# Delta rule: upper triangles of the decays by a selection by index on GpSimd, in place of products with a matrix of ones and zeros

## Chip, cores and metric

The kernel runs on one core of a Trainium2 chip. The metric is the device time of one execution in microseconds, as the median of several runs. One further execution was taken with the hardware profiler; its own time is given beside its span below, and all durations of single instructions come from it.

## What is computed

The program is a block of four residual layers on x of shape (8, 512, 256) in float32: a gated recurrence with an MLP, a mixture of experts, a gated delta rule and an attention over chosen tokens. The change touches the delta rule alone. There, for each batch and each of 8 heads (keys of 128, values of 64), the reference runs over 512 tokens

```python
def step(state, inp):
    q_t, k_t, v_t, a_t, b_t = inp
    retained = jnp.einsum('bhvk,bhk->bhv', state, k_t)
    rk = retained[..., None] * k_t[:, :, None, :]
    vk = v_t[..., None] * k_t[:, :, None, :]
    state = a4 * (state - b4 * rk) + b4 * vk
    o_t = jnp.einsum('bhvk,bhk->bhv', state, q_t)
```

with decays alpha = exp(g), where g is negative and comes from the token by a projection and a softplus; a4 and b4 are a_t and b_t with two axes added. Queries and keys are normed to length one, and the outputs are normed, gated and projected.

## The kernel before, in words

The tokens of a batch are cut into NT = 4 chunks of P = 128. Inside a chunk the recurrence is written with matrices: a strictly triangular matrix of key products, weighted by decays, is inverted, and the state is carried from chunk to chunk. Heads go in groups of HG = 4, so there are 16 groups (8 batches with 2 groups each), the loop over n near L1074.

The work of a group lies in generators, and a list of letters (`order`, L1059) says which generator is taken one step further at each point; in one turn of the loop over n, group n is advanced (`advance`, a; `sides`, v; `silus`, g; `outputs`, o), group n+1 is prepared and inverted (`prepare`, p; `inverses`, i), and the channels, norms and decays of group n+2 are made (`channels`, c; `norms`, n; `fade`, e). Rows of the next batch are loaded at even or odd n by `load` (t, l), which issues gathers from GpSimd (L1027) and adds them on VectorE (L1031). Each engine runs its own queue in order.

- `fade` (L721) makes, for each chunk t, the decays between all pairs of tokens of that chunk, for four heads side by side, in the tile e (128 partitions by 4 x 128). L728 on GpSimd multiplies le, which is one where the column is at or above the row and zero below, with g repeated along the columns. L730 on TensorE multiplies with gt (ones where the row is above the column), which sums g over the tokens between; L731 on ScalarE takes the exponential; L732 on GpSimd multiplies with le again, so that the lower triangle is zero. A group has four of each, so there are 64 of each in all.
- `prepare` (L736) multiplies the key and query products of a chunk (L746, TensorE) with e and a factor on VectorE (L748) and writes NQ. Its last reading of an e frees the tile for the group after.
- `inverses` (L751) inverts the triangular part of NQ. First blocks of 8 and 16 on VectorE, by many small instructions from SBUF to SBUF (L779, L789, L793, L794, L802, L803, L816, L817), then two transposes on VectorE (L763: dn and up), then larger blocks by matmuls on TensorE, from L831 on, which begin with dn.
- `advance` (L930) carries the state: products with the state (L950), VectorE (L952, L953), the product with the inverse (L957), ScalarE (L959), and the new state (L965 on GpSimd, L968 on TensorE, L970 or L972 on VectorE).
- `outputs` (L984) multiplies the gates with the outputs on GpSimd (L990).

The tile le is made once at the start of the program, by the operation that the change uses (`affine`, L69 and L70), and is also read by a matmul in `decays` (L666). Other uses of that operation are on tiles of 4, 8 and 128 elements with one loop in the pattern.

Of the kernel before, what the change touches and what calls it, by code (L numbers as in the profile page):

```python
# [16 lines left out]
ALU = mybir.AluOpType  # L17
# [3 lines left out]
P = 128  # L21
# [11 lines left out]
HG = 4  # L33
# [3 lines left out]
def bc(ap, axis, n):  # L37

    ap = ap.unsqueeze(axis)
    shape = list(ap.shape)  # L40
    shape[axis] = n
    return ap.to_broadcast(shape)
# [3 lines left out]
def block(ctx: ExitStack, tc: tile.TileContext, a: dict, out: bass.AP):  # L46
    nc = tc.nc
    V, S, G, TE = nc.vector, nc.scalar, nc.gpsimd, nc.tensor
# [4 lines left out]
    def cst(shape, name):  # L53
        return const.tile(shape, F32, name=name, tag=name)
# [18 lines left out]
    le = cst([P, P], "le")  # L73
# [492 lines left out]
    def delta_rule():  # L566
        with ExitStack() as cx:
# [153 lines left out]
            def fade(s):  # L721


                b, hg, hs = s.b, s.hg, s.hs
                s.es = []
                for t in range(NT):
                    e = un.tile([P, HG, P], F32, name=f"e{b}_{hg}_{t}", tag="e", bufs=NT)
                    G.tensor_mul(e, bc(le, 1, HG), bc(s.g[:, t, hs], 2, P))  # L728
                    pe = pa.tile([P, HG, P], F32, name=f"pe{b}_{hg}_{t}", tag="pa")
                    TE.matmul(pe, gt, e, start=True, stop=True)  # L730
                    S.activation(e, pe, AF.Exp)  # L731
                    G.tensor_mul(e, e, bc(le, 1, HG))  # L732
                    s.es.append(e)
                    yield

# [309 lines left out]
            def group(n):  # L1045

                b, hg = divmod(n, H1 // HG)
                return SimpleNamespace(**vars(seqs[b]), hg=hg, hs=slice(hg * HG, (hg + 1) * HG))
# [17 lines left out]
            for n in range(2):  # L1066
                s = groups[n] = group(n)
                drain(channels(s), norms(s), fade(s))
                if n == 0:
                    drain(prepare(s), inverses(s))  # L1070
# [3 lines left out]
            for n in range(total):  # L1074
                s, s1 = groups.pop(n), groups.get(n + 1)
# [316 lines left out]
```

## Time and profile before

| what | value |
|---|---|
| median of 3 runs | 3373.59 us (3373.55 to 3381.02) |
| the profiled execution | 3381.53 us, span 3379.8 us |
| mean granted TensorE clock | 0.910 |
| TensorE, VectorE, ScalarE, GpSimd busy | 3018.4, 1900.5, 1548.0, 574.0 us |
| delta rule, from first channels to last output | about 1490 to 2907 us of the span |
| L731, exponential on ScalarE, 128x512 | 64, mean 596 ns |
| L748, NQ on VectorE, 128x256 | 256, mean 477 ns |
| TensorE idle from 1545 to 2910 us, summed | 142.9 us |

How to read the lines of the profile: PE is TensorE, PEld its weight load, DVE VectorE, ACT ScalarE, POOL GpSimd. A row of a group gives line, engine, operation, output and inputs, shape and count, then the busy time in us and the mean of one in ns, and after the second bar the engine's idle time ahead of these instructions and what ended it. A row of the waits gives who waited for whom, the us in total, how often and the longest. A row of a timeline gives the start in us from the begin of the span, the duration of the merged piece, engine, line, operation and, in brackets, the idle time ahead of it with what ended it. Spans on GpSimd are rough.

### The profile page before, as it was taken

How to read it: one execution, taken by the hardware profiler on the slowest of the kernel's cores; microseconds unless marked ns; L12 is line 12 of the kernel's file. 1: busy time of each engine (PE TensorE's matmuls, PEld its weight loads, DVE VectorE, ACT ScalarE, POOL GpSimd, SP SyncE). 2: the span in 40 equal slices, each digit the busy share in tenths (PEclk: the TensorE clock that was granted, in tenths of full speed). 3: DMA queues.
4: the chain of work that ended last, by engine and by line, in shares of the span. 5: the costliest groups of instructions: out<-in, count | busy, mean ns of one | idle time of the engine just before them, and what ended most of it. 6: DMA issues, size and time to landing. Idle time of an engine off the chain costs nothing.

```text
span 3379.8 us, 59439 instructions
## 1 busy us (share of the span) xinstructions
PE 3018.4 (89%) x24662; PEld 2227.4 (66%) x24662; DVE 1900.5 (56%) x4415; ACT 1548.0 (46%) x2747; POOL 574.0 (17%) x629
## 2 busy tenths in 40 slices
PE   7999999979999999977899898898989999498887
PEld 3655555535999999973566666666666667365664
DVE  4555545534555555556467767767677664554432
ACT  3554442212333333325466666767666663233322
POOL 1000001320000111014122222312121110212111
PEclk8999998989999999998789898989989896698787
DMA  5000003220788888871000000000000000201111
GB/s 205 13 25 13 13 13 148 69 67 19 271 337 330 330 327 320 327 284 31 2 1 20 8 20 8 26 2 26 2 23 2 8 2 8 94 23 42 36 40 47
DMA packets 97133, 302.69 MB, mean 90 GB/s; under 512 B 12760, under 2 KB 79456, under 8 KB 87648
## 3 DMA queue, kind: packets, MB, share of 16 engines
q0 software_dynamic: 19440, 221.19, 17.4%
q1 hardware_dynamic: 68016, 68.44, 6.0%
q10 hardware_dynamic: 9408, 9.27, 0.8%
q8 instruction: 194, 3.18, 0.4%
q14 instruction: 75, 0.61, 0.1%
HBM read 248.79 MB, written 50.08 MB: 88 GB/s over the span
## 4 chain that ended last, share of the span: by engine, by line
PE 69%; DVE 12%; DMA 11%; issue 4%; ACT 2%; POOL 2%; SPq 0%; another core or an unknown queue 0%; ACTq 0%; POOLq 0%; DVEq 0%
PE p_r L444 13%; PE pc L681 8%; DMA zbuf<-bz,rows 5%; PE pp L304 3%; PE pk L746 3%; PE pj L399 3%; PE pyr L522 3%; PE pkq L950 3%; DMA w<-in_experts,wrow 2%; PE pf L394 2%; PE p_s L444 2%; PE py L1008 2%; PE st L1271 2%; PE pw L957 1%; DVE cy L685 1%
## 5 line engine op out<-in xcount | busy, mean ns | idle before, releaser
L444 PE MATMUL p_r<-zT,w 128*128 128x128 f32 x4544 | 533.0, 275 | 6.1 <-DMA w<-in_experts,wrow 5.5
L444 PEld LDWEIGHTS p_r<-zT,w 128*128 128x128 f32 x4544 | 525.0, 192 | 11.6 <-issue 7.1
L685 DVE SCALAR_TENSOR_TENSOR cy<-pc,conv,cy 128x509 f32<-128x509 f32 (+2 forms) x480 | 351.4, 740 | 139.7 <-ACT cy L683 134.6
L448 ACT ACTIVATE t_r<-p_r,w 128x128 f32<-128x128 f32 x568 | 170.9, 374 | 263.5 <-PE p_r L444 183.9
L444 PE MATMUL p_s<-sxT,shared_w 128*128 128x512 f32 x512 | 226.2, 603 | 22.1 <-DVE l_s L449 20.4
L444 PEld LDWEIGHTS p_s<-sxT,shared_w 128*128 128x128 f32 x512 | 98.1, 193 | 145.6 <-issue 106.3
L508 POOL DMA_INDIRECT w<-in_experts,wrow x71 | 66.8, 940 | 676.3 <-ACT sg_r L457 655.8
L449 DVE SCALAR_TENSOR_TENSOR l_r<-p_r,w,t_r 128x128 f32<-128x128 f32 x284 | 80.0, 344 | 175.7 <-PE p_r L444 175.7
L681 PE MATMUL pc<-cxT,wq 128*128 128x512 f32 x256 | 150.8, 714 | 15.0 <-DVE cy L685 12.9
L681 PE MATMUL pc<-cxT,wk 128*128 128x512 f32 x256 | 146.0, 665 | 6.1 <-DVE cy L685 3.7
L304 PE MATMUL pp<-hT,win 128*128 128x512 f32 x320 | 142.9, 598 | 0.2 <-ACT hT L126 0.2
L522 PE MATMUL pyr<-w,htr 128*128 128x256 f32 x568 | 136.0, 383 | 2.6 <-DVE htr L462 2.6
L683 ACT ACTIVATE cy<-pc,conv 128x512 f32<-128x512 f32 x160 | 108.4, 686 | 62.3 <-PE pc L681 61.0
L449 DVE SCALAR_TENSOR_TENSOR g_r<-p_r,w,t_r 128x128 f32<-128x128 f32 x284 | 79.9, 344 | 98.8 <-PE p_r L444 98.8
L746 PE MATMUL pk<-kq 128*128 128x256 f32 x512 | 130.2, 391 | 0.7 <-DVE NQ L748 0.4
L728 POOL TENSOR_TENSOR e<-le,g 128x512 f32<-128x512 f32 x64 | 66.3, 1042 | 364.2 <-DVE NQ L748 341.6
L748 DVE SCALAR_TENSOR_TENSOR NQ<-pk,nbk,e 128x256 f32<-128x256 f32 x256 | 110.0, 477 | 27.2 <-PE pk L746 26.8
L394 PE MATMUL pf<-hT,fc 128*128 128x512 f32 x256 | 121.5, 601 | 0.0
L457 ACT ACTIVATE sg_r<-g_r 128x512 f32<-128x512 f32 x71 | 44.8, 631 | 159.9 <-DVE g_r L455 159.9
L399 PE MATMUL pj<-pj,sT 128*128 128x256 f32 x512 | 113.1, 379 | 0.0
L522 PEld LDWEIGHTS pyr<-w,htr 128*128 128x128 f32 x568 | 103.6, 192 | 14.2 <-issue 2.7
L950 PEld LDWEIGHTS pkq<-state,kq 128*128 128x128 f32 x768 | 95.4, 197 | 24.2 <-DVE state L972 16.7
(393 smaller groups left out, 6179.0 us busy)
## 6 DMA issues: line engine op xcount, KB each, us to landing
zt<-zbuf SPq DMA_DIRECT2D x71, 128.0 KB
ybuf<-yt SPq DMA_DIRECT2D x71, 128.0 KB
zbuf<-zeros SPq DMA_DIRECT2D x11, 768.0 KB
x<-in_x SPq DMA_DIRECT2D x8, 512.0 KB
xbuf<-x SPq DMA_DIRECT2D x8, 512.0 KB
sx<-xbuf SPq DMA_DIRECT2D x8, 512.0 KB
xbuf<-sx SPq DMA_DIRECT2D x8, 512.0 KB
cx<-xbuf SPq DMA_DIRECT2D x8, 512.0 KB
```

Source lines behind the costliest of these rows:

```text
L304: TE.matmul(ps, win[:, k, m : m + P], hT[:, k, :], start=k == 0, stop=k == DK - 1)
L394: TE.matmul(ps, fc[:, k, f * P : (f + 1) * P], hT2[:, k, :], start=k == 0, stop=k == DK - 1)
L399: TE.matmul(ps, sT[:, f, t * P : (t + 1) * P], pj[:, f, :], start=f == 0, stop=f == 7)
L444: last_of[0] = TE.matmul(ps[:, f, :], wx[:, k, (f0 + f) * P : (f0 + f + 1) * P], xin[:, k, :], start=k == 0, stop=k == DK - 1)
L448: S.activation(t3[:, f, :], p3[:, f, :], AF.Identity, bias=b3[:, f0 + f : f0 + f + 1])
L449: V.scalar_tensor_tensor(t1[:, f, :], p1[:, f, :], b1[:, f0 + f : f0 + f + 1], t3[:, f, :], ALU.add, ALU.mult)
L522: last_of[0] = TE.matmul(ps, hT[:, f, :], w2[:, f, :], start=f == 0, stop=f == 3)
L681: TE.matmul(ps, w[:, k, n * P : (n + 1) * P], xT[:, k, :], start=k == 0, stop=k == DK - 1)
L685: V.scalar_tensor_tensor(y[:, j:], ps[:, : T - j], conv[:, at + n, 3 - j : 4 - j], y[:, j:], ALU.mult, ALU.add)
L746: TE.matmul(pk[:, j, :, :], kq[:, h + j, 0, ts], kq[:, h + j, :, ts], start=True, stop=True)
L748: V.scalar_tensor_tensor(NQ[:, :, t * HG + h + j, :], pk[:, j, :, :], s.nbk[:, t, h + j : h + j + 1], bc(e[:, h + j, :], 1, 2), ALU.mult, ...
L950: TE.matmul(ps[:, n, h, :], s.kq[:, h, n, ts], state[:, h, :], start=True, stop=True)
```

## The change

Both products with le become selections by index on GpSimd: element (p, h, j) of the output is the input where j - p is zero or more, and 0.0 elsewhere. The first reads g repeated along the columns by a zero step, the second works on e in place. Each now reads one tensor; before, each read two.

```diff
                 b, hg, hs = s.b, s.hg, s.hs
                 s.es = []
+
+                def upper(dst, src):
+
+                    G.affine_select(out=dst, in_=src, pattern=[[0, HG], [1, P]], compare_op=ALU.is_ge, fill=0.0, base=0, channel_multiplier=-1)
+
                 for t in range(NT):
                     e = un.tile([P, HG, P], F32, name=f"e{b}_{hg}_{t}", tag="e", bufs=NT)
-                    G.tensor_mul(e, bc(le, 1, HG), bc(s.g[:, t, hs], 2, P))
+                    upper(e, bc(s.g[:, t, hs], 2, P))
                     pe = pa.tile([P, HG, P], F32, name=f"pe{b}_{hg}_{t}", tag="pa")
                     TE.matmul(pe, gt, e, start=True, stop=True)
                     S.activation(e, pe, AF.Exp)
-                    G.tensor_mul(e, e, bc(le, 1, HG))
+                    upper(e, e)
                     s.es.append(e)
                     yield
```

## Prediction

> **What bounds the kernel now.** I read first the busy shares and the chain of waits on the page, then TensorE's waits inside the delta rule (1550 to 2760 us), then GpSimd's groups, then the timelines of two neighbouring steps of the group loop, engine beside engine.
>
> ```profile
> PE 3018.4 (89%) x24662; PEld 2227.4 (66%) x24662; DVE 1900.5 (56%) x4415; ACT 1548.0 (46%) x2747; POOL 574.0 (17%) x629
> ```
> TensorE is the bound and GpSimd, which alone is edited, is busy 17%. In the chain of the delta rule GpSimd stands only ahead of 1563 us (four L728 in a row, 4.02 us, and two gathers). Time saved on GpSimd itself is thus worth almost nothing; the question is what its instructions do to others.
>
> ```profile
> PE pn L831 <- DVE dn L763: 45.7, 6, 8.4
> ...
> PE pkq L950 <- DVE state L972: 11.2, 8, 1.6
> ```
> Both long waits of TensorE end at VectorE, in the inverses of the group ahead (L763 is their transpose) or behind them in VectorE's queue (L972). So I look at why VectorE is late there. A step whose turn loads rows (even n), first VectorE, then GpSimd, then TensorE:
>
> ```profile
> 2182.63 1.25 DVE L779 SCALAR_TENSOR_TENSOR L<-low,front 128x256 f32<-128x256 f32 x1
> ...
> 2186.96 1.83 DVE L793 TENSOR_TENSOR p<-L,inv 128x72 f32<-128x72 f32 x1
> ...
> 2194.28 1.22 DVE L816 TENSOR_SCALAR both<-inv,front 128x256 f32<-128x256 f32 x1
> 2195.42 1.35 DVE L817 TENSOR_SCALAR both<-inv,second 128x256 f32<-128x256 f32 x1
> ```
> ```profile
> 2182.32 1.27 POOL L732 TENSOR_TENSOR e<-e,le 128x512 f32<-128x512 f32 x1
> ...
> 2187.37 1.28 POOL L732 TENSOR_TENSOR e<-e,le 128x512 f32<-128x512 f32 x1
> ...
> 2194.07 2.54 POOL L732 TENSOR_TENSOR e<-e,le 128x512 f32<-128x512 f32 x2
> ```
> ```profile
> 2197.44 1.91 PE L831 MATMUL pn<-dn,NQ 32*32 32x16 f32 x128 [8.19 <-DVE dn L763]
> ```
> And the next step (odd n), VectorE and TensorE:
>
> ```profile
> 2259.27 1.07 DVE L793 TENSOR_TENSOR p<-L,inv 128x98 f32<-128x98 f32 x1
> ...
> 2260.66 1.84 DVE L802 TENSOR_TENSOR pm<-L,inv 128x512 f32<-128x512 f32 x1
> ...
> 2269.82 0.34 DVE L816 TENSOR_SCALAR both<-inv,front 128x256 f32<-128x256 f32 x1
> ```
> ```profile
> 2265.37 2.81 PE L950 MATMUL pkq<-state,kq 128*128 128x64 f32 x16 [1.58 <-DVE state L972]
> ```
> The same L816 takes 0.34 us where no L732 runs and 1.22 us beside one. Each of the long VectorE instructions ends 0.1 to 0.3 us behind the end of an L732 (2183.88 against 2183.59; 2188.79 against 2188.65; 2195.50 against about 2195.35): it doesn't run slowly, it stands until the product is done. Their clean times in the same views: L779 0.47, the 72-element L793 0.28, L816 and L817 0.34, the 98-element L793 0.32, pm 0.99. The lost time is 0.78 + 1.55 + 0.88 + 1.01 = 4.2 us in a full even step, and 0.5 (an 8-element L793, 0.73) + 0.75 + 0.85 = 2.1 us in an odd one; over the loop I count some 48 such cases and 41 us. VectorE instructions that read PSUM (L685, L748, L952) keep their times beside L732 and L728. That is the cost the edit can reach: not the product's own time but the time for which VectorE's SBUF-to-SBUF instructions stand.
>
> **The change, part by part.** It replaces 64 L728 and 64 L732 one for one. Built, the order of TensorE, VectorE, ScalarE and SyncE is the same instruction for instruction with the same waits, and GpSimd's too apart from the operation; no wait and no DMA is added or moved. The tile le stays (the matmul of L666 reads it).
>
> ```profile
> L732 POOL TENSOR_TENSOR e<-e,le 128x512 f32<-128x512 f32 x64 | 81.3, 1277 | 53.8 <-ACT e L731 53.7
> ...
> L728 POOL TENSOR_TENSOR e<-le,g 128x512 f32<-128x512 f32 x64 | 66.3, 1042 | 364.2 <-DVE NQ L748 341.6 <-DVE g L663 18.8 <-DVE mvc L110 2.6
> ...
> L1297 POOL COPY full<-den 128x512 f32<-128x512 f32 x16 | 9.3, 607 | 59.7 <-DVE den L1294 56.9 <-DVE ahead L1185 2.8
> ...
> L70 POOL TENSOR_SCALAR_AFFINE_SELECT heads<-heads 128x8 f32<-128x8 f32 x2 | 0.4, 200 | 0.0
> ...
> L70 POOL TENSOR_SCALAR_AFFINE_SELECT gt<-gt 128x128 f32<-128x128 f32 x1 | 0.3, 289 | 0.0
> ```
> Price of a new select. The trace has it at 8 and at 128 elements: (289 - 200)/120 = 0.74 ns an element, so 200 + 504 x 0.74 = 574 ns at 512. A one-input copy at 512 takes 607 ns, its source repeated by a zero step as g is here. I take 0.61. The old rows have one loop; the new pattern has two, [0,4] and [1,128]. If each row of 128 paid the whole price again it would be 4 x 289 = 1156 ns. Bounds: 0.57 and 1.16. The one rule that speaks against the change: the Trainium skill, "GPSIMD Engine Reference", Performance versus the Vector engine, puts data-dependent branching at about 12 cycles an element; at its 1.2 GHz that is an estimate of 5.1 us for 512 elements, four times the product, and over 100 us slower in all. The 0.74 ns slope is under one such cycle, so the operation does not branch by element; the row decides.
>
> Does it still make VectorE stand? The trace has no select beside an SBUF-reading VectorE instruction. The Trainium skill, "SBUF — State Buffer", SBUF: two separate sides, says that the pair of ports that VectorE and GpSimd share is locked for the whole instruction, against two-input or two-port VectorE instructions, by a GpSimd instruction that reads SBUF; a select reads SBUF, so by the rule the stall gets shorter, not nothing. Every stall above fits that. By the rule: 0.67 us off per L732 met. Without lock: all 4.2 and 2.1 us. I take the rule; the other end is a rival.
>
> Even step, walked through: L779 stands to the end of the first select. GpSimd reaches it 0.43 us earlier too (L728 ahead of it 1.04 to 0.61), so 0.78 is saved, all of the stall. L793 saves 0.67 of its 1.55. The gathers between wait for VectorE (L1031 frees their buffers) and shift with it. Then the pair: 2.54 becomes 1.22, and L816 and L817 end some 1.35 earlier. Sum 2.8 us, on the path: dn follows, and TensorE waits for nothing else (ScalarE's L814 waits for the same L803 and needs 0.62, less than L816 and L817 need). The gap of 8.2 becomes 5.4; next late is still dn. There are five such gaps (8.17, 8.38, 8.19, 8.17, 8.18): 14.0 us. A sixth, 4.64 with two stalls: 1.4. The first step, around 1705, with three stalls of 0.45, 0.50 and 0.86: 1.3.
>
> Odd step: the selects follow ScalarE's exponentials, not VectorE; VectorE gains some 0.5, 0.5 and 0.85 at its three stalls, 1.8 us at L972, more than the gap of TensorE ahead of L950 (1.29 once, 1.58 six times). The gaps close: 10.8 us. Next late is TensorE's own queue.
>
> Clock: behind four of these seven gaps the granted clock is at a half for 3.4, 3.4, 6.8 and 3.4 us (2266.35 to 2273.18 in the step shown, with TensorE busy throughout), 17 us that cost 8.5. If three quarters of that goes, 6 us. I add nothing behind the even gaps: 5.4 us of idleness will still halve the clock.
>
> Start: the four L728 at 1547.95 end 1.7 us earlier, but the gather behind them also waits for a VectorE L1031 that starts at 1551.04 (stands 0.74 us beside L728): 0.8 us.
>
> GpSimd's remaining saving, 81.3 + 66.3 - 128 x 0.61 = 69.5 us of busy time, is counted at nothing: it sits idle 364 us ahead of L728 alone. Nothing is queued later than before, so no cover is lost.
>
> Sum: 14.0 + 1.4 + 1.3 + 10.8 + 6 + 0.8 = 34 us. I take 32, as closed gaps may uncover a ScalarE wait (its table loads fill the odd step). The profiled execution took 3381.5 (span 3379.8 and 1.7 around it), so 3349.5 in its terms; it lies 8 us above the median of 3373.6, which gives 3342.
>
> **The rivals.**
> 1. The lock shortened, as above: 3342, some 12 to either side. Chance 0.62.
> 2. The select doesn't lock VectorE out, or more half-clock stretches vanish: even steps 5 x 4.2 + 1.8 + 1.7, odd 10.8, clock 8.5 and more, start 0.8, together about 47 to 55: 3318 to 3327. For it: no overlap was traced. Against: the rule, and the copy's like nature. Chance 0.13.
> 3. Little changes: the two-loop pattern restarts at each row and takes 1.16. Then 0.12 us goes from each L732 and 0.11 is added to each L728, which blocks nothing in the loop: 4 x 5 + 4 + 7 x 3 = 45 stalls on the path by 0.12, 5 us: 3368. A wait of ScalarE's in place of VectorE's would end near it. Chance 0.13.
> 4. Slower: the second loop is counted in software and costs at each element. From 1.28 us on, VectorE stands longer than today; 45 us of path for each further us of select. At 2.0 us it is 0.72 x 45 = 32 us: 3406. For it: no row has two loops. Against: the slope and the copy of 512 with two loops at 607. Chance 0.12.
>
> **How the numbers follow.** About 0.3%, 10 us, is what a measurement of this kernel can tell from no change. Rivals 1 and 2 are faster by more than that but for the upper edge of 1 (0.02): 0.73. Same: 0.13 and that edge, 0.15. Slower: 0.12. The range takes in 1 and 2 and the near part of 3: 3318 to 3366.
>
> **What would show it.** Right: select rows near 0.6 us in place of 1277 and 1042 ns; the 72-element L793 near 1.2 us, L817 near 0.9 or less; TensorE's wait for dn some 14 to 17 us less in total, that for L972 near nothing. Wrong: select rows above 1.1 us; or short rows and short VectorE instructions with TensorE waiting as long, for ScalarE. VectorE instructions at their clean times beside a select would say that there is no lock.

## The result and the profile after

| what | before | after |
|---|---|---|
| median of 4 runs each, same chip | 3375.74 us (3373.55 to 3381.02) | 3340.25 us (3335.47 to 3341.52) |
| ratio to before, 95% interval | 1 | 0.9892 [0.9876, 0.9907] |
| profiled execution, its span | 3381.53, 3379.8 us | 3341.52, 3339.8 us |
| mean granted clock | 0.910 | 0.915 |

The changed kernel is faster by 35.5 us; 3342 was forecast. Measured again beside the second group of experiments below, it gave 3337.39 us, 0.9894 [0.9875, 0.9913]. Its lines behind the edit stand five further down: L779 is now L784, L793 is L798, L802 is L807, L816 and L817 are L821 and L822, L831 is L836, L950 is L955, L763 is L768, L972 is L977, L1027 and L1031 are L1032 and L1036. Both selections have the line of their helper, L729; "e<-g" is the first, "e<-e" the second.

The busy line of the page, after:

```profile
PE 3002.4 (90%) x24662; PEld 2219.1 (66%) x24662; DVE 1864.6 (56%) x4415; ACT 1546.3 (46%) x2747; POOL 507.4 (15%) x629
```
The counts are the same. VectorE ran the same 4415 instructions in 36 us less: these are, to within a microsecond or two, the us for which they no longer stand (34.6 of them in the loop below). GpSimd is 67 us less busy. TensorE, with as many matmuls, is 16 us less busy, which I put down to its clock.

GpSimd's two groups, after:

```profile
L729 POOL TENSOR_SCALAR_AFFINE_SELECT e<-e 128x512 f32<-128x512 f32 x64 | 42.4, 669 | 66.4 <-ACT e L736 66.4
L729 POOL TENSOR_SCALAR_AFFINE_SELECT e<-g 128x512 f32<-128x512 f32 x64 | 40.2, 636 | 374.2 <-DVE NQ L753 351.8 <-DVE g L663 21.4
```
A selection takes 0.64 to 0.67 us where the products took 1.28 and 1.04. Neither of the dearer prices that the prediction weighed is seen: 1.16 us with a restart at each row of 128, or a price by element that would have made it 5.1 us.

The even step shown before, in the kernel after: VectorE, then GpSimd, then TensorE (timelines: start, duration, engine, line).

```profile
2169.31 0.48 DVE L784 SCALAR_TENSOR_TENSOR L<-low,front 128x256 f32<-128x256 f32 x1
...
2172.88 0.53 DVE L798 TENSOR_TENSOR p<-L,inv 128x72 f32<-128x72 f32 x1
...
2175.12 0.48 DVE L1039 SCALAR_TENSOR_TENSOR cx<-yg,wts,cx 128x256 f32<-128x256 f32 x1 [0.62 <-DMA yg<-ybuf,rows]
...
2179.82 0.57 DVE L821 TENSOR_SCALAR both<-inv,front 128x256 f32<-128x256 f32 x1
2180.31 0.72 DVE L822 TENSOR_SCALAR both<-inv,second 128x256 f32<-128x256 f32 x1
```
```profile
2168.59 0.63 POOL L729 TENSOR_SCALAR_AFFINE_SELECT e<-e 128x512 f32<-128x512 f32 x1
...
2172.29 0.97 POOL L1032 DMA_INDIRECT yg<-ybuf,rows  x1 [0.31 <-DVE p L798]
2173.27 0.64 POOL L729 TENSOR_SCALAR_AFFINE_SELECT e<-e 128x512 f32<-128x512 f32 x1
...
2179.62 1.27 POOL L729 TENSOR_SCALAR_AFFINE_SELECT e<-e 128x512 f32<-128x512 f32 x2
```
```profile
2181.70 1.90 PE L836 MATMUL pn<-dn,NQ 32*32 32x16 f32 x128 [5.77 <-DVE dn L768]
```
L784 is at its clean time, because the selection ahead of it ends at 2169.22, before L784 starts at 2169.31. L798 of 72 elements went from 1.83 to 0.53. L821 and L822 still stand, for 0.23 and 0.37 us, beside the two selections that end at 2180.89: VectorE still stands, for a shorter time. TensorE's gap went from 8.19 to 5.77. A new wait of 0.62 us for the landing of a gather is in VectorE's queue.

The odd step after, VectorE and TensorE:

```profile
2242.93 0.33 DVE L798 TENSOR_TENSOR p<-L,inv 128x98 f32<-128x98 f32 x1
...
2243.59 1.08 DVE L807 TENSOR_TENSOR pm<-L,inv 128x512 f32<-128x512 f32 x1
```
```profile
2247.82 1.89 PE L955 MATMUL pkq<-state,kq 128*128 128x64 f32 x16
```
Both long VectorE instructions (1.07 and 1.84 before) are clean or nearly so, and TensorE reaches L955 without a gap; the same sixteen matmuls take 1.89 us in place of 2.81, at full clock.

TensorE's waits from 1545 to 2730 us of the kernel after (us in total, times, longest), which takes in the same waits as the prediction's lines:

```profile
PE pn L836 <- DVE dn L768: 32.1, 7, 5.8
...
PE pkq L955 <- DVE state L977: 0.5, 1, 0.5
```
45.7 became 32.1 and 11.2 became 0.5. The five large gaps went from 8.17, 8.38, 8.19, 8.17 and 8.18 to 5.83, 5.74, 5.77, 5.75 and 5.75, the sixth from 4.64 to 2.95.

Last the loop as one stretch, from the first L831 of the first group to that of the fifteenth, before and after. The columns are the stretch, its length, TensorE's busy time, its weight loads, VectorE, ScalarE, GpSimd, the granted clock, the DMA share and GB/s.

```profile
1623.10:2754.00 1130.90, 1028.66 (x12571) 750.16 (x12571) 772.64 (x1633) 749.15 (x1105) 264.84 (x265) 0.91 0.04 11
```
```profile
1625.50:2723.20 1097.70, 1015.64 (x12566) 744.18 (x12566) 738.03 (x1633) 748.12 (x1105) 203.82 (x265) 0.92 0.04 11
```
The loop is 33.2 us shorter: TensorE is idle 20.2 us less (102.2 to 82.1) and busy 13.0 us less. By the slices of the clock, 213 us of the stretch ran at half clock before and 181 after. The stretch ahead of it, from the first channel matmul to the first L831, is 0.9 us shorter too (91.7 to 90.8), but it is 89.1 to 91.5 us in the other kernels of the first two groups below, with the old product there or without, so this is within its scatter. The stretch from the first L831 of the sixteenth group to the last output matmul is 7 us shorter (81.3 to 73.9), but that isn't the change's: see the first experiment.

### The profile page after: what moved, and what is told of

Read it like the earlier page. It is cut to its first block, busy times and chain, and to the rows that moved or that the text cites. A ratio compares the mean times of both kernels' runs of the same rounds, so it can differ in the third digit from the quotient of the medians.

```text
span 3339.8 us, 59439 instructions
## 1 busy us (share of the span) xinstructions
PE 3002.4 (90%) x24662; PEld 2219.1 (66%) x24662; DVE 1864.6 (56%) x4415; ACT 1546.3 (46%) x2747; POOL 507.4 (15%) x629
## 4 chain that ended last, share of the span: by engine, by line
PE 39%; DVE 7%; DMA 3%; issue 3%; ACT 2%; POOL 1%; another core or an unknown queue 0%; POOLq 0%; DVEq 0%; ACTq 0%; SPq 0%
PE pc L681 8%; PE pk L751 3%; PE pkq L955 3%; PE py L1013 2%; PE pg L929 2%; PE pw L962 2%; PE st L1276 1%; PE sc L1255 1%; PE pow L981 1%; PE pst L973 1%; PE pn L881 1%; PE pe L735 1%; PE pu L890 1%; PE pn L701 1%; DMA yg<-ybuf,rows 1%
## 5 line engine op out<-in xcount | busy, mean ns | idle before, releaser
L1255 PE MATMUL sc<-dk,dq 32*128 32x256 f32 x512 | 80.4, 532 | 30.0 <-DVE maxs L1257 25.8
L304 PEld LDWEIGHTS pp<-hT,win 128*128 128x128 f32 x320 | 60.1, 192 | 70.9 <-issue 66.5
```

The costliest lines, as they stand in the source:

```text
L304: TE.matmul(ps, win[:, k, m : m + P], hT[:, k, :], start=k == 0, stop=k == DK - 1)
L1255: TE.matmul(sc[r][:, j, :], qT[rs, 2 * m + j, qs], kT[rs, 2 * m + j, :], start=True, stop=True)
```

## The experiments

The theory: a GpSimd instruction that reads SBUF keeps some of VectorE's SBUF-to-SBUF instructions standing until it is done, so what counts is how long, and when, it runs beside the inverses. Those that stand in the traces are the ones with two inputs from SBUF (L779, L793, L802) and, with one input, L816, L817 and the copy L789. Transposes and reductions, with one input too, don't: in the kernel before, a transpose lies wholly beside a product and takes the 0.71 us that it takes elsewhere.

```profile
1702.03 0.71 DVE L763 STREAM_TRANSPOSE low<-own 128x512 f32<-128x512 f32 x1 [0.22 <-POOL own L776]
```
```profile
1702.02 1.04 POOL L728 TENSOR_TENSOR e<-le,g 128x512 f32<-128x512 f32 x1
```
The rivals: GpSimd's own time or its queue is what was saved; a part of the gain comes from the first selection; luck with the clock. Each kernel is measured against the kernel before on the same chip, whose medians were 3371.05 (first group), 3372.57 (second) and 3374.91 us (third).

| kernel | median us | ratio to before, 95% interval | loop, us | span, us |
|---|---|---|---|---|
| second selection only | 3340.11 | 0.9903 [0.9888, 0.9918] | 1096.2 | 3338.4 |
| first selection only | 3366.81 | 0.9987 [0.998, 0.9995] | 1128.0 | 3365.4 |
| no second mask | 3332.61 | 0.9884 [0.9866, 0.9901] | 1090.4 | 3330.9 |
| selection and two fills | 3332.9 | 0.9883 [0.9865, 0.9901] | 1094.4 | 3330.2 |
| second product late | 3336.32 | 0.9903 [0.9883, 0.9923] | 1091.9 | 3329.2 |
| second selection late | 3335.43 | 0.9896 [0.9879, 0.9913] | 1094.5 | 3333.5 |
| second selection twice | 3347.81 | 0.9927 [0.9911, 0.9944] | 1100.9 | 3342.3 |
| after, again | 3337.39 | 0.9894 [0.9875, 0.9913] | 1097.5 | 3338.5 |
| after, four gather buffers | 3325.45 | 0.9851 [0.9839, 0.9864] | 1095.8 | 3323.8 |
| before, four gather buffers | 3364.52 | 0.9971 [0.9959, 0.9984] | 1133.0 | 3364.7 |
| second late, four gather buffers | 3324.33 | 0.9861 [0.9845, 0.9877] | 1082.2 | 3319.2 |

"Loop" is the stretch of the last section, and "span" that of the whole program, in the profiled execution; the loop is 1130.9 before and 1097.7 after. The ratios are not the quotients of the two medians.

**One half at a time.** The second selection only:

```diff
-                    upper(e, bc(s.g[:, t, hs], 2, P))
+                    G.tensor_mul(e, bc(le, 1, HG), bc(s.g[:, t, hs], 2, P))
```


> Only the second product (on e in place, ahead of it the exponential) becomes a selection; the first stays a product with le. Theory of the held port (VectorE's SBUF-to-SBUF instructions stand while the second product runs): nearly the whole gain, 3340 to 3347 us, selects near 0.66 us, the first product at 1042 ns, the gap of TensorE ahead of the even steps' dn at 5.8 to 6.2 us and the odd steps' gap ahead of L950 gone. Rival, GpSimd's own time: of 65 us saved there 39 remain saved, so some 60% of the gain, about 3354. Rival, luck of the clock: no relation to which of the two is replaced.

And the first only:

```diff
-                    upper(e, e)
+                    G.tensor_mul(e, e, bc(le, 1, HG))
```


> Only the first product (on g) becomes a selection; the second stays a product of 1277 ns. Theory of the held port: the second product arrives up to 0.4 us earlier in five even steps and the start gains 0.8 us, so 3369 to 3376, within 0.3% of the kernel before, gaps of 7.7 to 8.2 us ahead of dn. Rival, GpSimd's own time: 26 of 65 us saved, 40% of the gain, about 3361.

The second alone gives the whole gain within its interval, and the loop too (1096.2 against 1097.7). The first alone gives 4 us, a little more than I expected (3366.81 against 3369 to 3376); its large gaps are 7.79 to 8.19, because the product behind it, which begins 0.4 us earlier, still ends late, and the gaps of the odd steps stay (11.3 us in the loop, 11.2 in the kernel before). So nearly all of the gain is the second selection's, behind the exponential and beside the inverses. In the profiled executions the stretch from the sixteenth group's first L831 to the last output matmul takes 81.3 us in the kernel before and 80.4 in the one with the second selection only, and 73.6 to 74.6 in all others of the first two groups, with the first selection only among them; 67 to 68 us of it are at half clock in the two long cases, 52 to 54 in the short ones. No selection and no product with le runs there. So these 7 us go with the clock and not with the edit. What decides between the two cases is not shown, and the spans of single profiles are good to 7 us.

**How much is left in the second mask.** The line is deleted; the lower triangles are then not zeroed.

```diff
-                    upper(e, e)
```


> The first is a selection, the second is left out (the lower triangles of the decays are then not set to zero, a part of the computation that is left away). No GpSimd instruction of the decays runs beside the inverses. Theory of the held port: what is left of the stalls beside the selects in the changed kernel (0.22 and 0.37 us at the pair ahead of dn in five even steps) goes too, the gathers are next late: 3335 to 3340. Rival, GpSimd's own time: another 42 us off it, 3315 to 3320.

By its ratio it can't be told from after (0.9884 against 0.9892 and 0.9894), and its median of 3332.61 us lies a little under the theory's 3335 and far above the 3315 to 3320 of GpSimd's own time. In the profile the loop is 7.3 us shorter, and the large gaps are 5.3 us but for one of 6.75 (such a one, 6.9, is in the second profile of the kernel after as well). So of the 40.5 us that the second mask costs the loop (1130.9 against 1090.4, with what the first selection gives) the cheaper operation already takes 33, some five sixths. Without a mask there the gaps are still 5.3 us: the rest of them is VectorE's own work and the gathers.

**Reading or only writing.** Behind each second selection GpSimd writes zeros over parts that are zero already:

```diff
+                    G.memset(e[96:128, :, 0:96], 0.0)
+                    G.memset(e[64:96, :, 0:64], 0.0)
```


> Both are selections, and behind each second selection two fills write zeros into parts of e that are zero already (rows 96 to 127, columns 0 to 95; rows 64 to 95, columns 0 to 63): together 0.6 to 0.75 us of GpSimd that only writes. GpSimd is as long at it as with the product. Theory of the held port, if only reading instructions hold it against two-input VectorE instructions: two-input ones (L779, L793, L802) keep their clean times beside a fill; only the two-port L816 and L817 could stand; 3340 to 3350. If a writing instruction holds it as well: 3355 to 3370. Rival, GpSimd's own time: the whole gain gone, 3370 to 3378.

GpSimd's groups, and then VectorE and GpSimd where the fills meet L786 (L784 of after, two lines down) and where they meet L824 (L822 of after):

```profile
L738 POOL MEMSET e<- 32x384 f32 x64 | 26.6, 416 | 3.7
L739 POOL MEMSET e<- 32x256 f32 x64 | 19.6, 306 | 2.4
```
```profile
2164.09 0.48 DVE L786 SCALAR_TENSOR_TENSOR L<-low,front 128x256 f32<-128x256 f32 x1
...
1777.48 0.58 DVE L824 TENSOR_SCALAR both<-inv,second 128x256 f32<-128x256 f32 x1
```
```profile
2164.08 0.41 POOL L738 MEMSET e<- 32x384 f32 x1
...
1777.47 0.44 POOL L738 MEMSET e<- 32x384 f32 x1
```
With 660 + 416 + 306 = 1382 ns a mask, GpSimd is as long in each as with the product (1277), and in the same place of its queue, and the kernel is as fast as after; its 3332.9 us lie a little under the 3340 to 3350 that I expected. GpSimd's own time and its queue are thus worth nothing that can be measured, and that rival falls. L786 starts 0.01 us behind the start of a fill of 0.41 and takes its clean 0.48, in all six even steps: a GpSimd instruction that only writes does not make a two-input instruction of VectorE stand. L824, which takes one input and is 0.35 where it is clean, does stand beside the fill, 0.23 us, and ends 0.15 behind it; in the loop this is the only time that it starts beside a fill. Both fit what the Trainium skill says in "SBUF — State Buffer", SBUF: two separate sides: VectorE's two-input instructions are shut out only by a GpSimd operation that reads SBUF, those in a two-port mode by any. That L824 runs in such a mode no trace here shows.

**The same product at another time.** If it is the meeting that costs, the old product may stay as it is, if it runs where no inverse does. From the third group on, the second product is taken out of `fade` and tied behind the transposes of the turn. The tie is a copy of one element of the transposed tile `up`, which is kept for it as `s1.up`:

```diff
-                    G.tensor_mul(e, e, bc(le, 1, HG))
+                    if b * (H1 // HG) + hg < 2:
+                        G.tensor_mul(e, e, bc(le, 1, HG))
...
+                if n + 2 < total:
+                    for e in groups[n + 2].es:
+                        G.tensor_copy(e[96:97, 0, 0:1], s1.up[96:97, 0, 0:1])
+                        G.tensor_mul(e, e, bc(le, 1, HG))
```


> Both operations are the products of the kernel before (1042 and 1277 ns), but for groups 2 to 15 the second product is tied behind the transposes of the inverses that are under way, so that it no longer runs beside them; the tie is a copy of one element of the transposed tile into an element of e that the product sets to zero, 56 copies of about 0.1 us. Theory of the held port: what counts is what runs beside the product, so nearly the whole gain without any selection: 3335 to 3350 us, VectorE's L779, L793, L802, L816 and L817 at their clean times. Rival, the operation itself is what counts: 3370 to 3380.

GpSimd and VectorE of this kernel, and VectorE's same instructions in the kernel after:

```profile
2183.72 5.16 POOL L1104 TENSOR_TENSOR e<-e,le 128x512 f32<-128x512 f32 x4
```
```profile
2180.92 0.35 DVE L821 TENSOR_SCALAR both<-inv,front 128x256 f32<-128x256 f32 x1
2181.19 0.35 DVE L822 TENSOR_SCALAR both<-inv,second 128x256 f32<-128x256 f32 x1
...
2187.13 2.70 DVE L1002 TENSOR_TENSOR gate<-gate,oms 128x256 f32<-128x256 f32 x4
```
```profile
2186.44 1.41 DVE L1002 TENSOR_TENSOR gate<-gate,oms 128x256 f32<-128x256 f32 x4
```
Four products in a row, 5.16 us, each as long as before: 3336.32 us, not to be told from the kernel after, though its runs spread more (3329.68 to 3347.74). L821 and L822 are clean. Not all of the stalls have gone: VectorE is busy 747.3 us in the loop, against 772.6 before and 738.1 after, and where it still stands it is for instance in L1002, 2.70 us in place of 1.41. TensorE hardly waits for it there: its waits for the gates are 1.3 us in the loop, 1.2 in the kernel after. This is the strongest of the runs. With the operation unchanged and only its place moved, the whole gain is there. The selection moved in the same way:

> Both selections, and the second tied behind the transposes in the same way. A version that may beat both kernels: the stalls of 0.22 and 0.37 us at the pair ahead of dn go, 5 to 6 us at most less than the changed kernel where it is not the gathers that are late: 3328 to 3336. Rival: the tie delays gates or gathers behind it on GpSimd's queue, or the selects now stand beside the outputs' VectorE instructions: 3335 to 3345.

It can't be told from after (3335.43 against 3337.39; the intervals overlap), though four of its large gaps are 5.3 against 5.8 (the fifth is 6.2) and the loop is 3 us shorter in the profile.

**Two selections for one.** The second selection is done twice, in place, which changes no value:

```diff
                    upper(e, e)
+                    upper(e, e)
```


> The second selection is done twice, one behind the other (the second time changes nothing), so GpSimd is as long at it as with the product, reading all the while, but in two pieces. Theory of the held port: two-input instructions slip in between or find the port free, the two-port L816 and L817 meet four selections in place of two and lose up to 1.2 us in five even steps: 3340 to 3352. If the pieces hold the port without a gap between them: 3360 to 3375, as before. Rival, GpSimd's own time: 3371.

VectorE beside the first pair of an even step, and GpSimd at that pair and at the end of the step:

```profile
2330.29 0.90 DVE L785 SCALAR_TENSOR_TENSOR L<-low,front 128x256 f32<-128x256 f32 x1
```
```profile
2329.57 1.34 POOL L729 TENSOR_SCALAR_AFFINE_SELECT e<-e 128x512 f32<-128x512 f32 x2
...
2340.98 2.49 POOL L729 TENSOR_SCALAR_AFFINE_SELECT e<-e 128x512 f32<-128x512 f32 x4
```
GpSimd is then a little longer (2 x 0.69 = 1.38 us) than with the product, but the kernel costs only 10.4 us over after by the medians, and not the 35 that the product costs on the same chip. In the profiled executions the loop is 3.4 us longer than after's, and VectorE is busy 750.3 us in it, a third of the way from 738.1 after to 772.6 before. The pair lasts from 2329.57 to 2330.91; L785 starts in the second of them, stands 0.42 us and ends 0.28 behind it. At the pair at the end of the step, where four selections lie in a row for 2.49 us, L822 and L823 (L821 and L822 of after) take 0.57 and 0.71, as with two: VectorE gets in between the selections. So what counts here is the length of one GpSimd instruction, not of the run of them.

**The kernel after, measured again** on the same chip as these three:

> The changed kernel once more, on the same chip as the other three: a ratio of 0.988 to 0.991 to the kernel before, some 3335 to 3341 us. By the rival of the clock's luck it would spread over more than 10 us around that.

The gain came again: 3337.39 us, a ratio of 0.9894, and all runs within 7 us (3333.45 to 3340.2). Luck with the clock does not explain that.

**The gathers.** The new wait for a gather's landing asked for more buffers:

```diff
-                        yg = un.tile([P, D], F32, name=f"yg{b}_{t}_{j}", tag="yg", bufs=2)
+                        yg = un.tile([P, D], F32, name=f"yg{b}_{t}_{j}", tag="yg", bufs=4)
```
In the kernel after:

> The changed kernel with four buffers for gathered rows in place of two, so that the gathers of the even steps are issued earlier. The order on the engines moves a little with it. Theory: in the changed kernel the landing of gathers is what comes next late in the even steps (VectorE waits 0.6 and 0.2 us for it between L798 and L799); with the rows there in time the gap ahead of dn falls from 5.75 to about 5 us in five steps: 4 us less, 3329 to 3337. Rival: the inverses' own chain sets the gap and the waits for rows were covered: within 2 us of the changed kernel.

In the kernel before, as a control:

> The kernel before, with products, and four buffers for gathered rows. Control for the one above: before the change the products made VectorE later than the rows, so that rows that come earlier should gain next to nothing: 3366 to 3376 us, gaps of 8 us ahead of dn. If it gains as much as the change or a large part of it, the gathers and not the held port were the cause.

And with the selection late as well:

> Both selections, the second tied behind the transposes, and four buffers for gathered rows: a version that may beat both kernels. Theory: the gap ahead of dn falls from 5.3 to about 4.5 us in five steps, 6 to 8 us less than the changed kernel: 3326 to 3334. Rival: no more than the selections alone, 3335 to 3341.

After with four buffers takes 3325.45 us, by the ratios 14 below after: a version that beats both kernels, by more than I expected. The gaps ahead of L836 fall from 5.8 to 4.0, 8.9 us in all. But little of the gain is there: the loop takes 1095.8 us against 1097.7, for TensorE is idle only 5.0 us less in it and busy 3.0 us more. Of the 16 us between the two profiles, 5.7 lie from the first channel matmul to the first L836 (85.1 against 90.8), 5.7 ahead of the first channel matmul, where the edit touches nothing, and 3.4 behind the last output matmul. The control makes the point sharper. TensorE's wait for dn and the loop in the kernel before with four buffers:

```profile
PE pn L831 <- DVE dn L763: 33.8, 6, 5.8
```
```profile
1615.80:2748.80 1133.00, 1031.11 (x12567) 751.08 (x12566) 770.50 (x1632) 749.63 (x1105) 259.56 (x263) 0.90 0.04 11
```
I expected its gaps to stay at 8 us, and that was wrong: they fell to 5.8, 11.9 us in all, as far as by the change. Yet the kernel's gain of 10 us lies ahead of the loop (82.4 against 91.7 us from the first channel matmul), and the loop is not shorter (1133.0 against 1130.9): TensorE is idle 101.9 us in it, against 102.2, for the wait has come back in several places (ScalarE's oq from 7.1 to 10.6, the product L957's wait for the inverse, 3.5, which was not there). VectorE's busy time in the loop is nearly what it was, 770.5 against 772.6: the stalls are nearly all there, and have only moved to other instructions of VectorE. For instance the 72-element L793 stands 1.0 us in the loop in place of 8.7, and L953 5.3 us in place of 0.8. The buffers change the order of the instructions, so which of them did it is not settled. With the late selection as well the loop does get shorter, 1082.2 us, by 9.5 us of idle time and 6 of busy time, and the gaps are 3.2 us; the median, 3324.33, can't be told from that of the four buffers alone.

With the four buffers in both kernels, the change is worth 3364.52 - 3325.45 = 39 us, about as without them.

## Why the prediction was right

The mechanism was the one named, and the sum came out: 33.5 us forecast for the loop with the clock (14.0 + 1.4 + 1.3 + 10.8 + 6), 33.2 measured. But the clock was put too low, and what came back of the closed gaps had no term; the two cancel.

- **Price of a selection.** 0.61 taken, 0.64 to 0.67 measured, close to the copy's row and to the slope. The estimate of 5.1 us from the 12 cycles an element for branching (the Trainium skill, "GPSIMD Engine Reference", Performance versus the Vector engine) does not apply to this operation: the row was the better guide.
- **Lock or no lock.** The rule was taken; the stalls are shorter and not gone (L821 and L822 above), and the late product and the fills show that it is the meeting with an instruction that reads, not GpSimd's time. That a pair of ports is behind it is the page's word, with which the fills agree. Of rival 2 the missing lock falls; its other half, 8.5 us or more of the clock, came true (13.0; its terms as listed add up to 44.6 us, so that its 47 to 55 asked for more still). Rivals 3 (a restart at each row) and 4 (a price by element) fall.
- **Even steps.** 2.8 us each forecast, 14.0 for five; the five gaps fell from 41.09 to 28.84, 12.3. L784 gave 0.77 (0.78 forecast). L798 of 72 elements gave 1.30 where 0.67 was forecast: the product came right behind the gather and L793 stood for its whole length as well, while with the selection VectorE waited only 0.25 us, to about the end of the gather. L821 and L822 gave 1.28 (1.35). Against these 3.4 us stands about 0.8 of new waits for landing gathers (0.62 in the lines above and 0.2 around L1036), which "next late is still dn" had left out. VectorE had been late enough to cover them.
- **The sixth gap and the first step** gave 1.7 and 1.45 us (1.4 and 1.3). **Odd steps**: 10.8 forecast, 10.7 measured (11.2 to 0.5). **Start**: 0.8 forecast, 0.9 measured, which confirms nothing: the stretch is 0.7 shorter with the second selection only too, where the product is still there.
- **The gaps closed, and some came back.** The terms above are 26.1 us, but TensorE's idle time in the loop fell by 20.2 only. By the waits of the loop, those for VectorE fell by 25.4 us (75.3 to 49.9), and those with no releaser in the profile rose by 6.3 (13.4 to 19.7), mostly ahead of L849. This rise is 4.6 us in the second profile of the kernel after and 1.7 with the second selection only; what L849 waits for is not shown. The prediction had no term for that, only a rounding from 34 to 32.
- **Clock.** 6 us forecast, 13.0 measured as busy time of the same matmuls; half clock fell by 32 us. The four stretches that I had counted, behind gaps that close, are 17 us of it, and all four are gone; I had counted nothing elsewhere. This and the step above cancel, within 1 us: that the total fits is partly luck. And the profiles differ by 7 us in the last group alone, with the clock.

The median moved by 35.5 us. How much of that is the last group's clock a median can't say; the loop's own 33 us, measured from the one profile of the kernel before, is in both profiles of the kernel after (1097.7 and 1097.5).

## What to carry to other kernels

What GpSimd costs is not its busy time but how long one of its reading instructions keeps some of VectorE's SBUF-to-SBUF instructions standing, above all those with two inputs; look for a VectorE instruction that takes longer beside GpSimd than the same one elsewhere, since neither waits nor chain show such a stall, and ask who waits for it. Such a stall can be shortened by an operation with one input in place of two, or moved to where no one waits, which gave as much here with the old operation. And a gap that gets smaller is not yet a gain: measure the idle time of the whole stretch, as the control with the four buffers shows.

## What was not expected

VectorE gets its turn between two GpSimd instructions that follow one another without a gap, but not always: directly behind a gather's issue the product went first (a stall of 1.55 us), the selection didn't (0.25). What decides this was not tried. A two-input VectorE instruction also seems to be let go before the selection beside it ends by the trace: in the kernel with the second selection only, L784 starts 0.31 us into a selection of 0.64 and takes 0.61 us, 0.13 over its clean time, where a wait for the whole would have cost 0.33, and ends 0.28 behind the selection, as L785 does with two of them; spans on GpSimd are rough, so this is no more than seen. And short gaps can go with half clock: of the seven gaps of 1.3 to 1.6 us ahead of L950 in the kernel before, four have a stretch of 3.4 or 6.8 us at half clock that begins within 2.2 us of their end, and three have none so near. In the kernel after, the gaps and these four stretches are gone.
